# A state-space scan in two halves: carrying the state through the first token's inputs instead of through the scan's initial value

## The chip, the cores and the metric

The kernel runs on one core of a Trainium2 chip. A core has a matrix engine (TensorE, PE in the profile), a vector engine (VectorE, DVE), a scalar engine (ScalarE, ACT), a general engine (GpSimd, POOL), and SyncE (SP), whose queue issues the DMA transfers here. Each engine works through its own instructions in order; between engines, semaphores order the work. The metric is device microseconds for one execution of the whole program, and the median over runs is what counts.

## The reference

The input is `x` of shape (16, 256, 32, 32): 16 images (batches) of 256 channels and 1024 tokens. Two layers follow one another, each with a group norm ahead and a residual around it. Layer 0 is a transformer block: position embedding, layer norm, attention with 4 heads of 32, a second layer norm and a small feed-forward. Layer 1 is a Mamba block with a gate, and its core is a recurrence over the tokens, for 512 inner channels `d` with 64 states `n` each:

```
delta = softplus(dt @ dt_proj_w.T + dt_proj_b)
A = -exp(A_log)
def step(h, inp):                       # once per token, h0 = 0
    d_t, B_t, C_t, u_t = inp
    dA = exp(d_t[..., None] * A)
    h = dA * h + (d_t * u_t)[..., None] * B_t[:, None, :]
    y = einsum('bdn,bn->bd', h, C_t)
```

Per batch that is 512 x 64 = 32768 recurrences of 1024 steps. Each step multiplies the state by a decay `dA`, and adds an input `delta * u * B`. Everything is computed in 32-bit floats, but for the exact three-piece split of `delta` in bfloat16 that the kernel makes for one matmul.

## The kernel before

**The scan.** A scan instruction of VectorE runs one recurrence per partition along the free dimension: `h[c] = a[c] * h[c-1] + v[c]`. A scan here covers 128 partitions (64 states of 2 channels, interleaved) and 512 tokens. So 1024 tokens take two halves `t = 0` and `t = 1`, and 512 channels take 256 scans in each half. A *unit* is two scans (`e = 0, 1`), that is four channels; a batch has 256 units in the order `t`, `k` (channel block of 128), `q` (of 32), `i` (of 4), and all 16 batches make 4096 units and 8192 scans. The second half has to go on from where the first ended: after the units of one `(k, q)` ScalarE copies the last column of its 16 scans into the tile `last` (L895), and the scans of `t = 1` name a column of `last` as their initial value.

**What a unit needs.** `load` issues a DMA on SP that brings `delta * u` of its four channels to all partitions as `dub` (L832; seven buffers, each set free by the scans of its unit). `inputs` multiplies it by `B` in place, once per `e`, on GpSimd (L842). `decay` has TensorE spread `delta` over the partitions into PSUM (`a`, L851; four buffers) and ScalarE take the exp with the scale `acol`, which holds `A` (L854). `scan` runs the two scans (L864). `outputs` contracts the states with `C` on TensorE (L901, L913), with ScalarE copies, and SP stores the result.

**The order.** A loop over the units writes the program out, and a pass at the end fixes that order on PE, ACT, DVE and POOL. In the turn of unit n it issues the load of unit n+6 (`AHEAD`), the multiplies of unit n+4 (`LEAD`), the scans of n, the decay of n+2, a share of the *side work*, and a step of the outputs that are running. The side work is everything else for the next batch (first norm, attention, and `scan_inputs`, which prepares the scan's operands and stores them in DRAM) and `gate_and_store` of the batch before. It is a generator whose steps carry weights, spread evenly over the units. The last batch has only a `gate_and_store` beside it. Before the first scan the first batch's preparation runs alone.

**Lines that the change and the prediction touch.** In `scan_inputs`, for each channel block `d`, `delta` of both halves is finished by two subtractions (L716), ScalarE casts its first piece (L717), `du` is formed and stored for the loads (L721, L722), and the pieces are stored as `dps` (L733), from which each `(k, q)` later loads `pieces` (L826). At the start, `vec` brings all per-channel constants in one DMA (L113), and `a_neg` is the exp of its `A_log` columns (L141), which becomes `acol`.

Of the kernel before, what the change touches and what calls it, by code (L numbers as in the profile page):

```python
# [11 lines left out]
F32 = mybir.dt.float32  # L12
BF16 = mybir.dt.bfloat16
AF = mybir.ActivationFunctionType
ALU = mybir.AluOpType
# [4 lines left out]
P = 128  # L20
# [8 lines left out]
DI = 512  # L29
ND = DI // P  # L30
NS = 64
# [4 lines left out]
SLOTS = 16  # L36
# [12 lines left out]
NV = _n  # L49
# [3 lines left out]
def attention_then_scan_kernel(  # L53
# [18 lines left out]
    nc = tc.nc  # L72
    B = x.shape[0]

    def pool(name, bufs, **kw):
        return ctx.enter_context(tc.tile_pool(name=name, bufs=bufs, **kw))

    const = pool("const", 1)
# [4 lines left out]
    small = pool("small", 2)  # L83
    dutp = pool("dutp", 7)
    blk = pool("blk", 2)
    hst = pool("hst", 1)
    dram = pool("dram", 2, space=DRAM)
# [14 lines left out]
    def work(name, n=L):  # L102
        return wide.tile([P, L + 2 + CONV], F32, name=name, tag="wide")[:, :n]

    def hwork(name):
        return half.tile([P, HL], F32, name=name, tag="half")

    def hs(h):
        return ts(h, HL)


    vec = const.tile([P, NV], F32, name="vec")
    nc.sync.dma_start(vec, vecs)  # L113

    def col(name, i=0, n=1):
        o, w = _COLS[name]
        assert i + n <= w
        return vec[:, o + i : o + i + n]
# [19 lines left out]


    a_neg = work("a_neg", ND * NS)  # L140
    nc.scalar.activation(a_neg, col("A_log", 0, ND * NS), AF.Exp)  # L141
    nc.vector.tensor_scalar(a_neg, a_neg, -1.0, None, ALU.mult)
    acol = const.tile([P, DI // 2], F32, name="acol")
    a2 = work("a2", 2 * P).rearrange("p (j n i) -> p j n i", j=2, i=2)
# [32 lines left out]
    t = work("ones_s")[:1]  # L177
# [3 lines left out]
    for k in range(KC):  # L181
        t = work("rel_s").rearrange("p (i j) -> p i j", j=32)
# [122 lines left out]
    state = [dict() for _ in range(B)]  # L305
# [231 lines left out]
    def scan_inputs(b):  # L537
        st = state[b]
# [25 lines left out]
        zs = dram.tile([DI, L], F32, name="zs", tag="zs")  # L564
# [9 lines left out]
        for d in range(ND):  # L574
            z = work("z")
            for hf in range(2):
# [7 lines left out]
                t = hwork("z_t")  # L584
# [6 lines left out]
        ud = dram.tile([DI, L], F32, name="ud", tag="ud")  # L591
        gs = dram.tile([C, L], F32, name="gs", tag="gs")
# [80 lines left out]
        rows = dram.tile([2 * NS, L], F32, name="rows", tag="rows")  # L673
# [2 lines left out]

        dps = dram.tile([ND * 3 * P, L], BF16, name="dps", tag="dps")
        dus = dram.tile([ND * NT * P, TB], F32, name="dus", tag="dus")  # L680
        dpv = dps.rearrange("(k q e p x) t -> k p e q x t", k=ND, q=4, e=2, p=3)
# [2 lines left out]
        def begin(d, hf):  # L684
            ps = psum("d_ps")
            nc.tensor.matmul(ps, wdt_s[:, ts(d, P)], dt[:RANK, hs(hf)], start=True, stop=True)
            e = hwork("sp_e")
            nc.scalar.activation(e, ps, AF.Abs, bias=col("dt_b", d))
            nc.scalar.activation(e, e, AF.Exp, scale=-1.0)
            return ps, e  # L690
# [11 lines left out]
        items = [begin(0, 0)]  # L702
        yield 1
        for d in range(ND):
            items = [more(d, *items[0]), begin(d, 1)]
            yield 1
            items[1] = more(d, *items[1])
            rest(*items[0])
            yield 1.4
            rest(*items[1])  # L710
            for ps, e, s in items:
                nc.scalar.activation(s, s, AF.Ln)
            yield 1.7
            pc = [ptp.tile([P, L], BF16, name="pc", tag="pt") for _ in range(3)]
            for hf, (ps, e, s) in enumerate(items):
                nc.vector.tensor_tensor(ps, s, ps, ALU.subtract)  # L716
                nc.scalar.copy(pc[0][:, hs(hf)], ps)  # L717
            yield 1.4
            du = work("du")
            for hf, (ps, e, s) in enumerate(items):  # L720
                nc.vector.tensor_tensor(du[:, hs(hf)], us[d][:, hs(hf)], ps, ALU.mult)  # L721
            nc.sync.dma_start(duv[d], du.rearrange("d (t c) -> d t c", t=NT))  # L722
            yield 1.4
            for hf, (ps, e, s) in enumerate(items):
                nc.vector.tensor_tensor(ps, ps, pc[0][:, hs(hf)], ALU.subtract)
                nc.scalar.copy(pc[1][:, hs(hf)], ps)
            yield 1.4
            for hf, (ps, e, s) in enumerate(items):
                nc.vector.tensor_tensor(pc[2][:, hs(hf)], ps, pc[1][:, hs(hf)], ALU.subtract)
            items, ps, e, s = [], None, None, None  # L730
            for p in range(3):
                for e in range(2):
                    nc.sync.dma_start(dpv[d, p, e], pc[p][e:P:2])  # L733
            if d + 1 < ND:
                items = [begin(d + 1, 0)]
            yield 1.4
        st.update(zs=zs, gs=gs, ud=ud, rows=rows, dps=dps, dus=dus)
        st["ys"] = dram.tile([DI, L], F32, name="ys", tag="ys")
        yield 1

# [2 lines left out]
    def gate_and_store(b):  # L743
# [61 lines left out]
    units = [  # L805
        (b, t, k, q, i)
        for b in range(B) for t in range(NT) for k in range(ND) for q in range(4) for i in range(8)
    ]
    blocks, loaded, decays = {}, {}, {}
    now = {}  # L810
# [27 lines left out]
    def inputs(n):  # L838
        b, t = units[n][:2]
        for e in range(2):  # L840
            v = loaded[n][:, e, :]
            nc.gpsimd.tensor_tensor(v, v, blocks[b, t]["bt"], ALU.mult)  # L842

    def decay(n):
        b, t, k, q, i = units[n]
        pieces = blocks[b, t, k, q]
        decays[n] = [aps.tile([P, TB], F32, name="a", tag="a") for _ in range(2)]
        for e in (1, 0):
            a, r = decays[n][e], ds(64 * e, 48)
            w = pick[r, i].rearrange("p n j -> p (n j)")  # L850
            nc.tensor.matmul(a, w, pieces[r], start=True, stop=True)  # L851
        for e, a in enumerate(decays[n]):
            at = 64 * k + 16 * q + 2 * i + e
            nc.scalar.activation(a, a, AF.Exp, scale=acol[:, at : at + 1])  # L854

    def scan(n, e):
        b, t, k, q, i = units[n]
        if (i, e) == (0, 0):
            if (t, k, q) == (0, 0, 0):
                now["last"] = blk.tile([P, DI // 2], F32, name="last", tag="last")  # L860
            now["h", q % 2] = hst.tile([P, SLOTS, TB], F32, name=f"h{q % 2}", tag=f"h{q % 2}")
        at = 64 * k + 16 * q + 2 * i + e
        first = now["last"][:, at : at + 1] if t else 0.0
        nc.vector.tensor_tensor_scan(  # L864
            now["h", q % 2][:, 2 * i + e, :], decays[n][e], loaded[n][:, e, :], first,
            ALU.mult, ALU.add,
        )
        if e == 1:
            del decays[n], loaded[n]
# [3 lines left out]
    def spread_c(b, t):  # L873
        if t == 0:
            now["cd"] = hst.tile([P, TB // 16, P], F32, name="cd", tag="cd")
            nc.gpsimd.memset(now["cd"], 0.0)
        ct = blocks[b, t]["ct"].rearrange("p (a c e) -> p a c e", c=4, e=4)
        for c in range(4):
            for j in range(2):
                nc.scalar.activation(  # L880
                    now["cd"][:, :, 40 * c + j : 40 * c + j + 7 : 2], ct[:, :, c],
                    AF.Identity, scale=par[:, j : j + 1],
                )
# [58 lines left out]
    for n in range(2):  # L942
        decay(n)
    running = []
    side, rate, due = iter(()), 0.0, 0.0
    for n, (b, t, k, q, i) in enumerate(units):
        at = n % UNITS
        if at == 0:
            parts = [prepare(b + 1)] if b + 1 < B else []
            total = steps * len(parts)  # L950
            if b > 0:
                parts = [first_norm(b + 1), gate_and_store(b - 1), attention_layer(b + 1), scan_inputs(b + 1)]
                if b + 1 == B:
                    parts = parts[1:2]
                total += GATE
            side = chain(*parts)
            rate, due = total / (UNITS - AHEAD - 3), 0.0
        if at == UNITS - AHEAD:
            for _ in side:
                pass  # L960
            if b + 2 < B:
                for go in fetches(state[b + 2].setdefault("x", []), x[b + 2]):
                    go()
        if n + AHEAD < len(units):
            load(n + AHEAD)
        if n + LEAD < len(units):
            inputs(n + LEAD)
        scan(n, 0)
        scan(n, 1)
        if n + 2 < len(units):  # L970
            decay(n + 2)
        if at >= (1 if b + 1 < B else 8):
            due += rate
            while due > 0.0:
                due -= next(side, 1e9)
        for g in list(running):
            if next(g, g) is g:
                running.remove(g)
        if i == 0 and n > 0:
            g = outputs(*units[n - 1][:4])  # L980
            next(g)
            running.append(g)
        if (k, q, i) == (0, 0, 6):
            spread_c(b, t)
    for g in running:
        for _ in g:
            pass
# [7 lines left out]
    last = {}  # L995
# [65 lines left out]
```

## Time and profile before

| | us |
|---|---|
| median of 3 runs | 13833.62 (13815.34 to 13842.49) |
| the profiled execution | 13784.86 |
| its span, first to last instruction | 13782.7 |
| first scan starts, last one ends | 392.9, 13737.4 |
| a usual batch, first half / second half (batch 5) | 416 / 431 |
| the last batch, first half / second half | 361 / 315 |

The halves are cut at the start of their first scan. In the profile a group is one line, engine and operation with its tiles and shapes; behind the count stand the busy time of the group, the mean length of one instruction in nanoseconds, and after the bar the time in which its engine was idle just before such instructions, with what ended that idle time. `x4096: 1157/1197/1226` gives a group's minimum, median and maximum in nanoseconds. A wait that several semaphores ended is put down to the one that came last by the profile, so the releaser named isn't always the true one. Some records are missing, so counts can be a few short.

### The profile page before, as it was taken

How to read it: one execution, taken by the hardware profiler on the slowest of the kernel's cores; microseconds unless marked ns; L12 is line 12 of the kernel's file. 1: busy time of each engine (PE TensorE's matmuls, PEld its weight loads, DVE VectorE, ACT ScalarE, POOL GpSimd, SP SyncE). 2: the span in 40 equal slices, each digit the busy share in tenths (PEclk: the TensorE clock that was granted, in tenths of full speed). 3: DMA queues.
4: the chain of work that ended last, by engine and by line, in shares of the span. 5: the costliest groups of instructions: out<-in, count | busy, mean ns of one | idle time of the engine just before them, and what ended most of it. 6: DMA issues, size and time to landing. Idle time of an engine off the chain costs nothing. (4 is left out here: it accounts for less than half of the span.)

```text
span 13782.7 us, 435036 instructions
## 1 busy us (share of the span) xinstructions
PE 11113.2 (81%) x185744; PEld 5728.7 (42%) x185744; DVE 12135.5 (88%) x11699; ACT 8088.7 (59%) x14245; POOL 10477.2 (76%) x8214
## 2 busy tenths in 40 slices
PE   7787878878787787978879788797887978878767
PEld 3344444444444444444444444444444444434434
DVE  3898898898898889888898888889888898888898
ACT  3666665656655565655656655566555655556644
POOL 0787777777787777777777787777777777777788
PEclk8686767867777686876767777677776776867767
DMA  1566566565665656556565565656656565565666
GB/s 55 196 207 230 187 214 208 201 222 196 211 207 199 218 201 223 194 199 218 197 231 186 197 226 191 232 185 202 219 191 230 187 214 205 194 228 187 209 219 223
DMA packets 964174, 2804.18 MB, mean 203 GB/s; under 512 B 138162, under 2 KB 285747, under 8 KB 962228
## 3 DMA queue, kind: packets, MB, share of 16 engines
q1 hardware_dynamic: 962228, 2776.34, 58.8%
q8 instruction: 1452, 23.79, 0.7%
q14 instruction: 494, 4.05, 0.1%
HBM read 2514.18 MB, written 261.62 MB: 201 GB/s over the span
## 5 line engine op out<-in xcount | busy, mean ns | idle before, releaser
L842 POOL TENSOR_TENSOR dub<-dub,bt 128x512 f32<-128x512 f32 x8192 | 10422.4, 1307 | 3254.5 <-DMA dub<-dus 2878.4
L854 ACT ACTIVATE a<-a,acol 128x512 f32<-128x512 f32 x8192 | 5064.9, 660 | 3728.2 <-PE a L851 3689.1
L864 DVE TENSOR_TENSOR_SCAN h<-a,last,dub 128x512 f32<-128x512 f32 x4096 | 4932.9, 1261 | 227.0 <-POOL dub L842 128.8
L864 DVE TENSOR_TENSOR_SCAN h<-a,dub 128x512 f32<-128x512 f32 x4096 | 4700.9, 1201 | 276.7 <-POOL dub L842 186.6
L851 PE MATMUL a<-pieces,pick 48*128 48x512 bf16 x8192 | 2914.9, 480 | 2103.1 <-DVE h L864 2037.8
L901 PEld LDWEIGHTS yb<-h,cd 128*32 128x32 f32 x131072 | 2677.2, 140 | 2166.2 <-issue 1847.3
L901 PE MATMUL yb<-h,cd 128*32 128x64 f32 x131072 | 3090.5, 265 | 160.9 <-DVE yb L891 115.9
L851 PEld LDWEIGHTS <-pick 48*128 48x128 bf16 x8192 | 498.0, 96 | 2507.4 <-issue 2293.2
L408 PE MATMUL s_ps<-ka,qa 32*128 32x512 f32 x2048 | 1115.7, 1009 | 23.2 <-DVE mx L399 15.2
L399 DVE TENSOR_REDUCE mx<-s_ps 128x1 f32<-128x512 f32 x1024 | 654.9, 678 | 279.0 <-PE s_ps L408 278.2
L913 PEld LDWEIGHTS yb<-turn,y 128*16 128x16 f32 x32768 | 418.9, 120 | 960.3 <-ACT y L909 484.6
L909 ACT COPY y<-yb 128x256 f32<-128x256 f32 x1024 | 383.4, 374 | 693.6 <-PE yb L901 688.3
L913 PE MATMUL yb<-turn,y 128*16 128x32 f32 x32768 | 555.2, 216 | 193.8 <-ACT y L909 173.0
L444 PE MATMUL st_ps<-qa,ka 33*128 33x512 f32 x2048 | 590.2, 613 | 25.9 <-ACT pt L452 25.5
L432 PE MATMUL av<-pt,vv 128*64 128x512 f32 x2048 | 572.7, 635 | 4.3 <-ACT sums L390 3.3
L452 ACT ACTIVATE pt<-st_ps 128x512 f32<-128x512 f32 x1024 | 558.9, 609 | 28.8 <-PE st_ps L444 28.4
L408 PEld LDWEIGHTS s_ps<-ka,qa 32*128 32x128 f32 x2048 | 345.4, 274 | 402.3 <-DVE mx L399 221.4
L630 PE MATMUL g_ps<-w,xp 128*128 128x256 f32 x1536 | 475.2, 468 | 0.0
L630 PEld LDWEIGHTS g_ps<-w,xp 128*128 128x128 f32 x1536 | 401.9, 329 | 137.6 <-issue 92.6
L789 PE MATMUL m_ps<-w,xs 128*128 128x256 f32 x1024 | 316.7, 459 | 10.9 <-DVE xs L764 10.9
L921 ACT COPY yo<-yb 128x256 f32<-128x256 f32 x512 | 193.1, 377 | 222.2 <-PE yb L913 219.7
L615 DVE SCALAR_TENSOR_TENSOR u<-up,cwh,u 128x1024 f32<-128x1024 f32 x192 | 300.9, 1567 | 23.8 <-ACT u L607 23.6
(135 smaller groups left out, 7593.8 us busy)
## 6 DMA issues: line engine op xcount, KB each, us to landing
dub<-dus SPq DMA_DIRECT2D x4096, 512.0 KB
dps<-pc SPq DMA_DIRECT2D x384, 128.0 KB
pieces<-dps SPq DMA_DIRECT2D x1024, 48.0 KB
xs<-in_x_dram SPq DMA_DIRECT2D x64, 512.0 KB
xs<-kept SPq DMA_DIRECT2D x64, 512.0 KB
zs<-z SPq DMA_DIRECT2D x64, 512.0 KB
ud<-u SPq DMA_DIRECT2D x64, 512.0 KB
dus<-du SPq DMA_DIRECT2D x64, 512.0 KB
```

What stands on the lines that cost most here:

```text
L399: nc.vector.tensor_reduce(mx[:, e, c, hf : hf + 1], s, AX.X, ALU.max)
L408: nc.tensor.matmul(s, qa[r, ts(c, P)], ka[r, hs(hf)], start=True, stop=True)
L432: nc.tensor.matmul(av[ts(e, 2 * DH)], vv[j // (NJ // 2)][:, j % (NJ // 2), 2 * pair + e, :], pts[e], start=(j == 0), stop=(j == NJ - 1),)
L444: nc.tensor.matmul(s, ka[r, ts(j, P)], qa[r, hs(hf)], start=True, stop=True)
L452: nc.scalar.activation(pt, s, AF.Exp)
L630: nc.tensor.matmul(ps[:, ts(q, C)], xp[k][:, ds(first + t, P, 4)], wg_s[:, k, t, :], start=(i == 0), stop=False,)
L842: nc.gpsimd.tensor_tensor(v, v, blocks[b, t]["bt"], ALU.mult)
L851: nc.tensor.matmul(a, w, pieces[r], start=True, stop=True)
L854: nc.scalar.activation(a, a, AF.Exp, scale=acol[:, at : at + 1])
L864: nc.vector.tensor_tensor_scan(now["h", q % 2][:, 2 * i + e, :], decays[n][e], loaded[n][:, e, :], first, ALU.mult, ALU.add,)
L901: nc.tensor.matmul(yb[ts(g, 32), ts(s, 64)], cd[:, at // 16, ts(c, 32)], hbuf[:, :, at : at + 4], start=(c == 0), stop=(c == 3),)
L913: nc.tensor.matmul(out4[32 * s : 32 * s + 16, half, e], y2[:, 64 * s + e : 64 * s + 64 : 4], turn[:, e], start=True, stop=True,)
```

## The change

All scans start from the constant 0.0. What the initial value did for the second half is done by its first token's input instead: for `h[0] = a[0] * last + v[0]` the product `a[0] * last` is added to `v[0]` ahead of the scan. So the kernel needs the decay of token 512 for every channel and state. `scan_inputs` has ScalarE copy `delta` of that token for each block of 128 channels, and stores it in a small DRAM tensor `d0`. In the batch's own turn, while the first half is scanned, two DMAs spread `d0` over the partitions as `ea`, GpSimd multiplies it by `acol`, and ScalarE takes the exp (at the first units of `k = 1` with `q = 0, 1, 2`). In the second half GpSimd multiplies 16 columns of `ea` and `last` into `on` for each `(k, q)`, and adds two columns of it to the first token of `dub` for each unit, after the unit's two multiplies.

The space for `ea` comes from `vec`, which no longer holds the `A_log` columns: these are loaded straight into `a_neg`, by a DMA of their own.

```diff
+    NC = NV - ND * NS
+    vec = const.tile([P, NC], F32, name="vec")
+    nc.sync.dma_start(vec, vecs[:, :NC])
...
     a_neg = work("a_neg", ND * NS)
-    nc.scalar.activation(a_neg, col("A_log", 0, ND * NS), AF.Exp)
+    nc.sync.dma_start(a_neg, vecs[:, NC:])
+    nc.scalar.activation(a_neg, a_neg, AF.Exp)
...
+        d0 = dram.tile([DI, 1], F32, name="d0", tag="d0")
+        dcol = small.tile([P, ND], F32, name="dcol", tag="dcol")
...
                 nc.vector.tensor_tensor(ps, s, ps, ALU.subtract)
                 nc.scalar.copy(pc[0][:, hs(hf)], ps)
+            nc.scalar.copy(dcol[:, d : d + 1], items[1][0][:, :1])
+            nc.sync.dma_start(d0[ts(d, P), :], dcol[:, d : d + 1])
             yield 1.4
...
             nc.gpsimd.tensor_tensor(v, v, blocks[b, t]["bt"], ALU.mult)
 
+        if t == 1:
+            k, q, i = units[n][2:]
+            if i == 0:
+                at = 64 * k + 16 * q
+                now["on"] = small.tile([P, SLOTS], F32, name="on", tag="on")
+                nc.gpsimd.tensor_tensor(
+                    now["on"], now["ea"][:, ds(at, SLOTS)], now["last"][:, ds(at, SLOTS)], ALU.mult
+                )
+            v = loaded[n][:, :, 0]
+            nc.gpsimd.tensor_tensor(v, v, now["on"][:, ds(2 * i, 2)], ALU.add)
...
-        at = 64 * k + 16 * q + 2 * i + e
-        first = now["last"][:, at : at + 1] if t else 0.0
         nc.vector.tensor_tensor_scan(
-            now["h", q % 2][:, 2 * i + e, :], decays[n][e], loaded[n][:, e, :], first,
+            now["h", q % 2][:, 2 * i + e, :], decays[n][e], loaded[n][:, e, :], 0.0,
             ALU.mult, ALU.add,
         )
...
+        if (t, k, i) == (0, 1, 0):
+            if q == 0:
+                now["ea"] = hst.tile([P, DI // 2], F32, name="ea", tag="ea")
+                src = state[b]["d0"].rearrange("(m j s) x -> j m (s x)", m=16, j=2)
+                for j in range(2):
+                    nc.sync.dma_start(
+                        now["ea"][j:P:2].rearrange("p (m s) -> p m s", m=16),
+                        src[j].unsqueeze(0).to_broadcast([NS, 16, 16]),
+                    )
+            elif q == 1:
+                nc.gpsimd.tensor_tensor(now["ea"], now["ea"], acol, ALU.mult)
+            elif q == 2:
+                nc.scalar.activation(now["ea"], now["ea"], AF.Exp)
```

More of the change, by code (lines that the diff above doesn't have):

```diff
@@ L109, in hs @@
         return ts(h, HL)
-    vec = const.tile([P, NV], F32, name="vec")
-    nc.sync.dma_start(vec, vecs)
+    NC = NV - ND * NS
+    vec = const.tile([P, NC], F32, name="vec")
+    nc.sync.dma_start(vec, vecs[:, :NC])
     def col(name, i=0, n=1):
@@ L736, in scan_inputs @@
             yield 1.4
-        st.update(zs=zs, gs=gs, ud=ud, rows=rows, dps=dps, dus=dus)
+        st.update(d0=d0, zs=zs, gs=gs, ud=ud, rows=rows, dps=dps, dus=dus)
         st["ys"] = dram.tile([DI, L], F32, name="ys", tag="ys")
```

## The prediction

> **What bounds the kernel now.** First the page: busy shares and the cost of the groups; for the two scan rows I took the answer by form, which names every releaser.
>
> ```profile
> PE 11113.2 (81%) x185744; PEld 5728.7 (42%) x185744; DVE 12135.5 (88%) x11699; ACT 8088.7 (59%) x14245; POOL 10477.2 (76%) x8214
> ...
> L842 POOL TENSOR_TENSOR dub<-dub,bt 128x512 f32<-128x512 f32 x8192 | 10422.4, 1307 | 3254.5 <-DMA dub<-dus 2878.4
> ...
> L864 DVE TENSOR_TENSOR_SCAN h<-a,last,dub 128x512 f32<-128x512 f32 x4096 | 4932.9, 1261 | 227.0 <-POOL dub L842 128.8 <-issue 94.5
> L864 DVE TENSOR_TENSOR_SCAN h<-a,dub 128x512 f32<-128x512 f32 x4096 | 4700.9, 1201 | 276.7 <-POOL dub L842 186.6 <-issue 83.4 <-ACT a L854 1.4
> ```
>
> The reader is to see that VectorE (DVE) is the fullest engine, that 9633.8 us of its 12135.5 are scans, and that the scans which name `last` (second half of the tokens) are 60 ns longer on average than those that start from the constant. GpSimd (POOL) comes next; its idle time is mostly waiting for loads, whose buffers only finished scans set free. Then the scan line alone:
>
> ```profile
> L864 DVE TENSOR_TENSOR_SCAN h<-a,dub x4096: 1157/1197/1226, 392.9 to 13421.2; 128x512 f32<-128x512 f32 x196
> L864 DVE TENSOR_TENSOR_SCAN h<-a,last,dub x4096: 1153/1257/1285, 780.2 to 13736.1; 128x512 f32<-128x512 f32 x196
> ```
>
> The medians (third field: min/median/max) differ by 60 ns and each form is narrow, so the 60 ns belong to the form, not to some disturbed stretch. Whether they are real pace or only a longer record, the timeline tells, from unbroken rows of scans and multiplies (start, length, count):
>
> ```profile
> 4013.33 11.25 DVE L864 TENSOR_TENSOR_SCAN h<-a,dub 128x512 f32<-128x512 f32 x10 [1.27 <-POOL dub L842]
> ...
> 13639.61 10.65 DVE L864 TENSOR_TENSOR_SCAN h<-a,last,dub 128x512 f32<-128x512 f32 x9
> ...
> 13639.91 11.20 POOL L842 TENSOR_TENSOR dub<-dub,bt 128x512 f32<-128x512 f32 x9
> ```
>
> Less one scan, over the steps between: (11.25-1.20)/9 = 1.117 us from the constant, (10.65-1.26)/8 = 1.174 us from `last`, so 57 ns of pace. A multiply: (11.20-1.27)/8 = 1.241 us. A unit (two of each) is 2.23 or 2.35 us of DVE and 2.48 us of POOL. Where DVE does scans alone, POOL is already the slower of the two. So the last view is by stage: batch 5's second half, its first 16 units, and batch 15's second half (us, then busy of each engine, PE's granted clock, DMA).
>
> ```profile
> 4988.20:5419.00 430.80, 332.99 (x5684) 173.92 (x5684) 393.06 (x369) 263.03 (x450) 318.35 (x249) 0.74 0.61 205
> ...
> 4988.40:5033.50 45.10, 37.05 (x717) 17.36 (x715) 43.44 (x41) 31.37 (x62) 40.68 (x34) 0.81 0.62 210
> ...
> 13422.30:13737.40 315.10, 235.67 (x5437) 139.11 (x5436) 307.93 (x267) 174.89 (x311) 303.16 (x246) 0.70 0.66 226
> ```
>
> A usual second half is DVE's (393 of 431 us; POOL 318). The last one, with no next batch to prepare, is a tie (308 and 303 of 315, ten POOL records missing).
>
> **What the Trainium skill says.** "VectorE: DVE Perf Modes", section "Scalar operands", says that a scalar is a constant in the instruction or a [P, 1] operand read per partition; it prices neither, this trace does. "SBUF — State Buffer", section "Who interferes with whom", says that a VectorE instruction with one SBUF input doesn't contend with GpSimd and one with two does; the scan reads `a` from PSUM, and the narrow spread of both forms beside a busy POOL agrees. "GPSIMD Engine Reference", section 3.1, has 4497 ns for an fp32 tensor_tensor of 2048 elements. No run here has a short one.
>
> **The change part by part.** *Scans.* 4096 lose 60 ns: 245.8 us at most. 256 of them are in the last half, counted below; 3840 give 15 x 15.4 = -230 us.
>
> *The small adds.* 2048 of 128x2 and 256 multiplies of 128x16 on POOL; none is in the trace. From 1.241 us at 512 elements and the skill's 4.497 us at 2048: 2.12 ns an element, 0.156 us fixed, so an estimate of 0.16 us. The add reads what the multiply before it wrote, and may wait for it to end: up to one overlap more, 1.271-1.241 = 0.03. I take 0.20 for both kinds (0.25 for the multiply). Below: 0.10, the 128x1 memset on POOL (99 to 103 ns). Above: 0.40, the 294 ns of the 128x128 select in the preamble and 0.1 for a wait on each side. A usual half then needs 318 + 128x0.2 + 16x0.25 = 348 us of POOL in about 418: hidden under DVE. If the cover were gone it would be 30 us a half. No scan starts until the add of its unit is done; multiplies are issued four units ahead, so that is late only where POOL has no lead.
>
> *Where it has little.* The first 8 units of a second half fall in the attention's value phase, with no VectorE work but scans: POOL 8 x 2.68 = 21.4 us against DVE 8 x 2.23 = 17.9. The difference, 3.6 us, comes partly out of the lead; I charge half, 1.8 x 15 = +27.
>
> *The last half.* POOL sets it: 128 x 2.48 + 26 + 4 = 347 us, less the four units that it is ahead at the start (10), so 337 and a scan pair: about 338 against 315.1, +23. At 0.10 it is +10, at 0.40 +50.
>
> *Waits on other engines.* Where VectorE waits for an answer of PE or ScalarE asked for a unit earlier (the waits for `z_t`, `d_ps`, `ln_v`, `ln_m`, `gn_v_ps`: about 16 in a second half), a unit shorter by 0.12 us is a wait longer by as much: 16 x 0.12 x 15 = +29.
>
> *ScalarE.* Per batch four 128x1 copies, at most 0.22 each (the 128x16 copy of `last` takes 0.217), and one exp of 128x256 (0.42, the row at L141): 1.3 us on an engine 59% busy. It runs beside other exps, so no table load. Hidden.
>
> *DMA and its queue.* Four stores of `d0` a batch, each of 128 pieces of 4 bytes. Each waits on SP for a ScalarE copy behind two casts behind two 0.68 us VectorE subtractions: the next `dub` load is issued some 2.3 us later, and `pieces` behind it. Four of 256 loads; they come six units (20 us) before their scan, and the store of `du` blocks the queue likewise today. Two loads of `ea` a batch, 2048 pieces of 64 bytes; the skill ("DMA: Bandwidth & Descriptors", "Specifications") wants 512 bytes for full rate. No run shows this one; from 0 to 8 us of queue, at a unit where POOL is waiting for loads anyway. The `ea` multiply on POOL takes 256 x 2.12 ns + 0.16 = 0.70 us. Together I charge 0.6 us a batch, +10; 0 to 60 is the range.
>
> *Preamble.* `a_neg` gets its own DMA: 0.4 us of SP issue and perhaps a microsecond of landing, +1.
>
> Sum: -230 + 27 + 23 + 29 + 10 + 1 = -140. The profiled span of 13782.7 (13784.9 with what lies around it) becomes 13643. The runs' median, 13833.6, lies 49 us above that execution; I take the 140 from it: 13693.
>
> **The rivals.** *All of it hidden* (adds of 0.10, no lengthened waits): -230 + 10 + 5 = -215, about 13620. For it: VectorE is 91% busy in these halves. Against it: the last half can't gain.
>
> *The chain scan, PE `a`, exp, scan takes over.* A scan's end frees the PSUM buffer that PE refills and ScalarE turns into the decay two units on. If it has too little slack, a wait takes the place of the 60 ns: with half of the gain left, and the 29 of lengthened waits within the other half, -115 + 61 = -54, about 13780. For it: PE is 81% busy at a clock of 0.73. Against: scans waited 1.4 us in all for that exp.
>
> *GpSimd becomes the bound, slower than before.* Place: the small add; price: from 0.65 us each. At that price a usual half needs 318 + 83 + 11 = 412 us of POOL, level with DVE's 415, stretches without VectorE side work go over and eat some 10 of the 15.4 us, and the last half loses 128 x 0.65 + 11 - 10 = 85, which is what the 15 others then gain. At 0.8 us: POOL needs 434 in each of 15 halves (3 more than now and bursts of 5), the last +105: +225, about 14060. For it: an instruction of two elements is all fixed cost, and two dependences per unit. Against: memsets of 0.1 us.
>
> *The 60 ns aren't the operand's*: then only costs remain, +60, 13890. The first-half scans, which are the new form exactly, speak against it.
>
> **How the numbers follow.** Chances: forecast 0.68 (13640 to 13750), all hidden 0.14, chain 0.08, GpSimd bound 0.07, not the operand 0.03. Leaving out the last two, half the chain's and a third of the first rival's gives 13625 to 13775. Within 0.2% of 13834 (28 us, about what this kernel's measurement can tell) lies some half of the chain's case and a little of GpSimd's: 0.05. Faster 0.87, slower 0.08.
>
> **What would show it.** One scan group of 8192 with mean near 1201 ns; a 128x2 add row near 0.2 us; second halves near 419 us, the last near 338 with scans waiting for the add; first halves unchanged. An add above 0.4 us, or scans waiting for `a`, would make the forecast wrong.

## The result and the profile after

The changed kernel takes 13928.94 us (median of 4 runs, 13919.26 to 13938.57) against 13838.06 for the kernel before (4 runs). The ratio is 1.0067, with a 95% interval of 1.0050 to 1.0085: it is slower by about 93 us, where 13693 was forecast. The profiled execution has a span of 13936.7 us, 154.0 above that of before.

First the page of the changed kernel (busy shares), its scan line, and the answer by form for its GpSimd instructions. As in before's rows, the bar parts busy time and mean from the idle time just ahead.

```profile
PE 11167.3 (80%) x185744; PEld 5754.2 (41%) x185744; DVE 11952.6 (86%) x11699; ACT 8103.0 (58%) x14325; POOL 10982.3 (79%) x10534
...
L879 DVE TENSOR_TENSOR_SCAN h<-a,dub x8192: 1153/1198/1226, 428.7 to 13890.1; 128x512 f32<-128x512 f32 x200
...
L859 POOL TENSOR_TENSOR dub<-dub,on 128x2 f32<-128x2 f32 x2048 | 475.8, 232 | 160.5
L855 POOL TENSOR_TENSOR on<-ea,last 128x16 f32<-128x16 f32 x256 | 60.7, 237 | 0.0
L1010 POOL TENSOR_TENSOR ea<-ea,acol 128x256 f32<-128x256 f32 x16 | 11.7, 730 | 0.0
```

All scans now have a median of 1198 ns: the 60 ns are gone, as forecast. VectorE is busy 183 us less, and not the 246 of 4096 times 60 ns: the scans' own rows give 215 (9633.8 us before, 9418.5 now), and its other instructions grew by 32 us, for a reason that no run isolates. The small adds take 232 ns and 78 ns of idle time ahead of each (160.5 us over 2048), so some 0.27 us once the overlap of 0.046 us between neighbouring records is taken off; 0.20 was forecast. In the trace, a unit whose multiplies follow one another without waiting takes GpSimd 2.45 us without an add and 2.72 with one, the same 0.27. The time is longer for all that. The stages, cut as before (us, then busy of PE, PE's weight loads, DVE, ACT, POOL; PE's granted clock, DMA share, GB/s): the second half of batch 5, its last 16 units and the last half, first before (whose last half stands in the prediction), then after.

```profile
4988.36:5419.49 431.13, 333.23 (x5685) 173.87 (x5683) 393.19 (x369) 263.36 (x450) 318.68 (x250) 0.74 0.61 205
...
5377.84:5419.49 41.65, 29.86 (x672) 17.08 (x672) 41.29 (x39) 22.75 (x42) 31.76 (x27) 0.62 0.76 267
```

```profile
5080.04:5514.14 434.10, 333.31 (x5684) 173.92 (x5682) 378.52 (x369) 263.98 (x454) 354.62 (x391) 0.74 0.64 203
...
5466.25:5514.14 47.89, 33.53 (x671) 17.82 (x671) 40.29 (x39) 23.37 (x43) 40.48 (x47) 0.50 0.66 238
13543.73:13891.35 347.62, 253.76 (x5437) 143.66 (x5436) 303.96 (x267) 175.46 (x311) 334.70 (x392) 0.64 0.62 205
```

VectorE has 14.7 us less to do in the half, and the half is 3 us longer; its last 16 units alone are 6.2 us longer, at a lower transfer rate (238 GB/s for 267). The last half grew from 315.0 to 347.6 us and is GpSimd's now. The 154 us of the two profiles lie so, by the starts of the scans: before the first scan +35.8; batch 0's halves +12.8 and +2.3; the 14 first halves of batches 1 to 14 +1.7 each (+23), the 14 second halves +4.0 each (+57); batch 15 -9 and +33.

Of the 35.8 us ahead of the first scan, some 21 are not the change's. In the first 300 us TensorE was granted 0.83 of its clock in the profile of before and 0.76 in this one, and executions of other kernels here start near one or the other as well. The row kernel below, whose start is the same but for the stores, had 0.84 and its first scan at 393.6; without adds, which this stretch doesn't have, it had 0.76 and 414.1. So 14 to 15 us of it are left for the stores, and totals of single executions are compared with care.

Then the queue that issues the transfers (SP), at the same step of the preparation of batch 0, before and after:

```profile
376.36 0.38 SPq L722 DMA_DIRECT2D dus<-du  x1
376.83 6.07 SPq L733 DMA_DIRECT2D dps<-pc  x6
```

```profile
404.98 0.33 SPq L723 DMA_DIRECT2D d<-dcol  x1
406.22 0.38 SPq L728 DMA_DIRECT2D dus<-du  x1
407.45 12.06 SPq L739 DMA_DIRECT2D dps<-pc  x6
```

The six stores of `dps` behind a store of `d0` take 12.06 us to issue instead of 6.07. The transfer queue of the whole run, before and after (packets, MB, share of the 16 DMA engines):

```profile
q1 hardware_dynamic: 962228, 2776.34, 58.8%
```

```profile
q1 hardware_dynamic: 1004868, 2778.48, 61.9%
```

By the trace, packets were in flight for 8623 us of all 16 engines instead of 8110. The 2 MB more are the loads of `ea`; the 64 stores bring 0.03 MB. If all of the 513 us were theirs, it would be 8 us for each; the experiments will put it at some 6. The waits of SP name them too: in the changed kernel it waited 67.5 us at the loads of `dub` and 46.7 at the stores of `dps` for the landing of `d<-dcol`.

### The profile page after: what moved, and what is told of

It reads as the page before. It is cut to its first block, busy times and chain, and to the rows that moved or that the text cites. A ratio compares the mean times of both kernels' runs of the same rounds, so it can differ in the third digit from the quotient of the medians.

```text
span 13936.7 us, 435942 instructions
## 1 busy us (share of the span) xinstructions
PE 11167.3 (80%) x185744; PEld 5754.2 (41%) x185744; DVE 11952.6 (86%) x11699; ACT 8103.0 (58%) x14325; POOL 10982.3 (79%) x10534
## 5 line engine op out<-in xcount | busy, mean ns | idle before, releaser
L879 DVE TENSOR_TENSOR_SCAN h<-a,dub 128x512 f32<-128x512 f32 x8192 | 9418.5, 1203 | 665.2 <-issue 236.4
L446 PE MATMUL st_ps<-qa,ka 33*128 33x512 f32 x2048 | 604.5, 625 | 27.1 <-ACT pt L454 26.5
L859 POOL TENSOR_TENSOR dub<-dub,on 128x2 f32<-128x2 f32 x2048 | 475.8, 232 | 160.5
```

Of the source, the lines that this page charges most:

```text
L446: nc.tensor.matmul(s, ka[r, ts(j, P)], qa[r, hs(hf)], start=True, stop=True)
L879: nc.vector.tensor_tensor_scan(now["h", q % 2][:, 2 * i + e, :], decays[n][e], loaded[n][:, e, :], 0.0, ALU.mult, ALU.add,)
```

## The experiments

Theory S puts the loss to the 4-byte stores of `d0`, and otherwise keeps the forecast. Rival G puts it to GpSimd's adds and the scans' waits for them. Rival C is the chain of the forecast's rivals: a shorter scan only waits longer for TensorE and the exp.

**The stores as one row.** The store in the channel loop goes; behind the loop:

```diff
-            nc.sync.dma_start(d0[ts(d, P), :], dcol[:, d : d + 1])
...
+        row = psum("d0_ps", 1)
+        for d in range(ND):
+            nc.tensor.matmul(row[:, ts(d, P)], dcol[:, d : d + 1], ident, start=True, stop=True)
+        drow = hwork("drow")[:1]
+        nc.scalar.copy(drow, row)
+        nc.sync.dma_start(d0, drow)
```

> The changed kernel, but the first-half delta column of a batch is turned into one row by four tiny TensorE matmuls and stored with a single contiguous 2 KB DMA, instead of four stores of 128 pieces of 4 bytes. Theory S (each 4-byte store stops the DMA rings for some 7 us, and the loads behind it come late): 64 stops go, the rest of the forecast's sum holds, so about 120 us below the kernel before (80 to 160), first scan within 5 us of 393, DMA share back near 59%. Rival G (GpSimd's adds and the scans' waits for them ate the gain): the stores do not matter, still some 60 to 90 us above the kernel before. Rival C (faster scans only wait longer for TensorE and ScalarE): within 30 us of the kernel before.

Measured: 13771.78 us against 13809.7, ratio 0.9977 (0.9968 to 0.9987). The first scan starts at 393.6. From 1.0067 to 0.9977 is 0.90%, some 124 us, and it falls where the stores were. But S is only half right: 32 us of gain, not 120, which is close to the 30 that rival C allowed.

**The stores alone.** The kernel before, with these two lines in the channel loop and nothing that reads `d0`:

```diff
+            nc.scalar.copy(dcol[:, d : d + 1], items[1][0][:, :1])
+            nc.sync.dma_start(d0[ts(d, P), :], dcol[:, d : d + 1])
```

> The kernel before plus only the ScalarE copy of a delta column and its 4-byte store, four per batch; nothing reads what is stored. Theory S: 36 us before the first scan, 13 in the first half of batch 0, and some 6 to 10 in each of 14 second halves, together 120 to 200 us above the kernel before. Rivals G and C, and the forecast's own term: the stores are hidden, at most 15 us above.

Measured: ratio 1.0081 (1.0058 to 1.0105), some 112 us, for four small copies and four stores a batch. DMA share 61.7%. The expected 120 to 200 took the 21 us of TensorE's clock for the stores'; without them the total lies in the range, but a second half is longer by 3.5 us (433.2 for 429.7) and not by the 6 to 10 expected, so what a stop costs depends on the work around it. G and C fall as explanations of the slowdown.

**Without the adds.** The row kernel, less the adds:

```diff
-            nc.gpsimd.tensor_tensor(v, v, now["on"][:, ds(2 * i, 2)], ALU.add)
```

> The row store, with the 2048 small GpSimd adds left out, so the second half does not receive the carried state (that part of the computation is missing); scans start from the constant. Theory S: the full gain of the scans less the lengthened waits, 180 to 220 us below the kernel before, and 30 to 60 below the row store with adds, mostly in the last half. Rival G: this one alone is fast, more than 150 below the row store. Rival C: within 50 us of the kernel before.

Measured: 13711.69 us, ratio 0.9935 (0.9919 to 0.9950), some 90 us below, where 180 to 220 were expected. The scans are as short as they can be here (mean 1201 ns), GpSimd has no adds, the stores are gone, and less than half of the scans' time comes back. S is right with 30 to 60 us below the row store (it is 58) and wrong with its gain; G wanted more than 150 below the row store, and C at most 50 below the kernel before. The stages say where. Mean us of these units over batches 1 to 14, from the starts of the scans:

| units of a batch | before | changed | row | row, no adds | selective (below) |
|---|---|---|---|---|---|
| 128 to 135 | 19.9 | 19.9 | 19.9 | 19.9 | 20.0 |
| 136 to 143 | 26.3 | 28.7 | 28.5 | 28.4 | 26.6 |
| 144 to 191 | 176.2 | 171.2 | 171.4 | 170.8 | 171.1 |
| 192 to 215 | 83.3 | 82.8 | 82.8 | 82.6 | 83.9 |
| 216 to 239 | 82.4 | 83.2 | 80.3 | 80.3 | 80.3 |
| 240 to 255 | 41.6 | 48.0 | 42.7 | 40.8 | 42.3 |
| second half | 429.7 | 433.8 | 425.5 | 422.8 | 424.1 |

Every 8 units hold 16 scans, so 0.96 us could be gained there. Without adds, units 144 to 191 give 5.4 us of 5.8, units 216 to 239 give 2.1 of 2.9, and units 240 to 255 give 0.9 of 1.9; the first 8 give nothing, units 136 to 143 lose 2.1 (3.1 with what they should have gained), units 192 to 215 give 0.7 of 2.9. 6.9 us of 15.4 are left. Kernels whose second halves differ only by stores that stop nothing (below) have 429.5 to 430.3 us for 429.7, so a few tenths are spread. The changed kernel's column differs from the row's from unit 216 on, by 8.2 us: there the channel blocks' stores of `d0` stand, and the loads of the next batch wait behind them.

Why the first 8 units give nothing shows in the timeline of the kernel without adds, in batch 5, by engine (start, length, what, idle time ahead and its releaser): VectorE, then ScalarE, TensorE and GpSimd.

```profile
5010.30 2.34 DVE L885 TENSOR_TENSOR_SCAN h<-a,dub 128x512 f32<-128x512 f32 x2 [0.20 <-issue]
5013.52 2.34 DVE L885 TENSOR_TENSOR_SCAN h<-a,dub 128x512 f32<-128x512 f32 x2 [0.89 <-POOL dub L854]
```

```profile
5012.44 0.37 ACT L930 COPY y<-yb 128x256 f32<-128x256 f32 x1 [0.66 <-PE yb L922]
5012.77 2.39 ACT L877 ACTIVATE a<-a,acol 128x512 f32<-128x512 f32 x4
```

```profile
5009.31 1.02 PE L446 MATMUL st_ps<-qa,ka 33*128 33x512 f32 x4
5010.27 1.08 PE L434 MATMUL av<-pt,vv 128*64 128x512 f32 x4
5011.27 1.10 PE L922 MATMUL yb<-h,cd 128*32 128x64 f32 x64
5012.31 0.39 PE L874 MATMUL a<-pieces,pick 48*128 48x512 bf16 x2
```

```profile
5010.60 4.97 POOL L854 TENSOR_TENSOR dub<-dub,bt 128x512 f32<-128x512 f32 x4 [0.72 <-DMA dub<-dus]
```

The scans at 5013.52 waited 0.89 us, put down to POOL. But TensorE worked without a gap from the attention's `st_ps` and `av` to `yb`; only then came `a` (5012.31 to 5012.70), though the scan that frees its buffer, four scans back, had ended at 5008.98. The exp behind it began at 5012.77, its first instruction takes 0.66 us, and the scan followed 0.09 us after. The scan's own multiply had ended 10.7 us earlier. The releaser named is the wrong one, and it is so nearly everywhere. In batches 1 to 14 of this kernel the scans idled 501 us; 498 of them ended within 0.15 us of the end of the scan's own exp, and 0.4 within 0.15 us of the end of its own multiply. For the kernel before it is 437 of 452 us for the exp, and none for the multiply. That the exp came last is thus counted; why it came late is shown by the timeline for this one place.

**The adds alone.** The kernel before, with adds of zero in the same place:

```diff
+        if t == 1:
+            v = loaded[n][:, :, 0]
+            nc.gpsimd.tensor_tensor(v, v, zero, ALU.add)
```

> The kernel before plus 2048 GpSimd adds of zero of the same shape and place, scans still from the kept state. Theory S: hidden in 15 second halves (at most 2 us each), and about 30 in the last one, so 25 to 60 us above the kernel before. Rival G: 150 us or more above. Rival C says nothing on this one.

Measured: ratio 1.0017 (1.0010 to 1.0024), 23 us. A second half takes 430.1 us for 429.7, the last one 344.3 for 315.0. So the adds are hidden but in the last half. Beside the faster scans they cost more: from 0.9935 without them to 0.9977 with them is 58 us; in the profiles 27 us in the last half and 2.7 in each of the 14 others. That is near the 50 us that the forecast charged for adds (27 and 23), so G doesn't explain the missing gain either.

**What stops the transfers.** The kernel before again with the stores alone, once into rows that lie 512 bytes apart, once with pieces of 64 bytes:

```diff
-        d0 = dram.tile([DI, 1], F32, name="d0", tag="d0")
+        d0 = dram.tile([DI, P], F32, name="d0", tag="d0")
...
-            nc.sync.dma_start(d0[ts(d, P), :], dcol[:, d : d + 1])
+            nc.sync.dma_start(d0[ts(d, P), :1], dcol[:, d : d + 1])
```

```diff
+        d0 = dram.tile([DI, 16], F32, name="d0", tag="d0")
+        dcol = small.tile([P, ND, 16], F32, name="dcol", tag="dcol")
...
+            nc.scalar.copy(dcol[:, d], items[1][0][:, :16])
+            nc.sync.dma_start(d0[ts(d, P), :], dcol[:, d])
```

> The kernel before plus the 4-byte stores, but each of the 128 pieces goes to its own 512-byte row of DRAM. Theory L (the stop comes from many short writes into the same few hundred bytes): the stop is gone, transfer in the ten microseconds behind a store as ahead of it (about 200 GB/s), time within 20 us of the kernel before. Theory P (short pieces stop the rings wherever they go): as with the packed store, 50 to 140 GB/s in the bins 2 to 10 us behind it, and 90 to 140 us above the kernel before.

> The kernel before plus four stores a batch of 128 pieces of 64 bytes, packed (8 KB). Theory L: eight pieces share 512 bytes instead of 128, so the stop shrinks to a small part, at most 30 us above the kernel before. Theory P: half or more of the packed 4-byte store's 110 us stays, since a piece of 64 bytes is still short.

One execution each gave 13837.11 and 13825.98 us beside one of the kernel before of 13765.14, outside what L had said; yet no stop showed. So both were run again, 12 times each.

> The 4-byte stores into rows 512 bytes apart, timed: one look put it 72 us above one look of the kernel before, though no stop shows behind the stores. Theory L: the difference was the spread of single runs, so within 25 us of the kernel before. Theory P: 90 to 140 us above, and the stop is hidden from the packets' times.

> The packed stores of 64-byte pieces, timed. Theory L: within 30 us of the kernel before. Theory P: 55 us or more above.

Measured: ratios 1.0003 (0.9995 to 1.0012) and 1.0010 (0.9996 to 1.0024); DMA share 59.3% in both. The same number of packets (971444 in the whole run) costs nothing measurable with rows of their own, and 112 us packed into 512 bytes. Packets were in flight 404 us of all 16 engines longer with the packed store (8593 for 8189), 6.3 us for each of the 64. Three stretches of 3 us, from 3 to 12 us behind the same store (the second of the four in batch 4's turn), show it, with the columns of the stages above (the last two are the DMA share and GB/s): the changed kernel, then the rows 512 bytes apart.

```profile
4558.30:4561.30 3.00, 2.92 (x66) 1.80 (x66) 3.00 (x5) 2.23 (x4) 2.92 (x5) 0.50 1.64 152
4561.30:4564.30 3.00, 2.56 (x68) 1.80 (x66) 3.00 (x4) 1.24 (x2) 2.52 (x3) 0.50 0.78 128
4564.30:4567.30 3.00, 2.82 (x14) 0.73 (x12) 3.00 (x4) 1.99 (x4) 1.46 (x2) 0.50 0.67 122
```

```profile
4520.20:4523.20 3.00, 2.54 (x66) 1.80 (x66) 3.00 (x5) 1.92 (x4) 0.00 (x0) 0.50 0.98 287
4523.20:4526.20 3.00, 2.43 (x58) 1.49 (x60) 3.00 (x3) 1.55 (x3) 2.49 (x2) 0.50 0.98 357
4526.20:4529.20 3.00, 3.00 (x29) 0.87 (x21) 3.00 (x5) 1.61 (x3) 2.01 (x2) 0.50 0.71 239
```

About half the rate or less, with a share that goes over 1 in one stretch: packets stay in flight for longer. On the mean over all 64 stores, the rate from 6 to 10 us behind the store's issue is 47 GB/s in the changed kernel and 304 with the rows apart, while the engines are as busy in both (0.94 and 0.89). From 2 us before a store to 12 us after it, 37 packets longer than 0.7 us begin on the mean, against 6 with the rows apart; the longest takes 6.3 us in the median store, against 1.1.

**TensorE relieved.** To see whether TensorE sets the pace at units 192 to 207, where the gate's convolution runs, two kernels with a third of its matmuls: the kernel before, and the row kernel without adds.

```diff
-            for i in range(3 * KC):
+            for i in range(2):
```

> The kernel before with only 2 of the 6 matmuls of each gate convolution block (the gate's other taps and channels are missing from the result). It is the control for the next one. If TensorE sets the pace at units 192 to 207 of a batch, these 16 units get shorter (55.3 us before) by a microsecond or more.

> The row store without the adds (the carried state is missing), with the same 2 of 6 gate matmuls. Theory C (behind a full TensorE the exp comes late, so a shorter scan only waits): with TensorE relieved the scans' 0.96 us per 8 units come back at units 192 to 207, 1.5 us or more for the 16 units against the control, where it was 0.4 with all six matmuls; elsewhere no change. Rival W (the wait there is another engine's or a fixed latency): still at most 0.7.

Measured in one execution each, for units 192 to 207 (mean of batches 1 to 14): 55.3 us before, 52.9 in the control; 54.9 without adds, 51.0 with TensorE relieved as well. The shorter scan is worth 0.4 us with all matmuls and 1.9 with a third of them. At units 184 to 191, the convolution's start, it goes from 1.1 to 1.8. So TensorE holds back gain here, as C said, and W's at most 0.7 is missed. But the rest of C's picture isn't shown: at units 200 to 207 alone the control has 24.8 us and so has the other, and all 1.9 us came at 192 to 199, where the scans alone save 0.96. TensorE was also relieved by less than the edit suggests. For units 192 to 207 of batch 5, before and in the control:

```profile
5211.83:5267.27 55.44, 48.27 (x766) 30.37 (x766) 51.30 (x43) 27.59 (x49) 43.93 (x32) 0.94 0.63 206
```

```profile
5220.62:5272.47 51.85, 46.62 (x726) 24.21 (x725) 48.56 (x42) 27.38 (x48) 43.59 (x31) 0.73 0.67 219
```

The granted clock fell from 0.94 to 0.73, and TensorE's busy time hardly did. For a whole second half, the shorter scan is worth 8.5 us with TensorE relieved (425.8 less 417.4) and 6.9 without, so this stage accounts for some 1.5 of the 8.5 us that are lost.

For units 136 to 143 no run was made for this alone; their wait is for the transfer of the softmax sums. VectorE waited for it 26.5 us in the kernel before, 23.4 with the adds alone and 29.3 in the selective kernel below, which all keep the old scans there, and 63.2, 59.0 and 60.2 in the changed, the row and the row kernel without adds. So the wait follows the shorter scans, not the adds; why it grows by more than they save is open.

**A version that beats both.** The row store; the zero start and its add only where the table shows a gain, and elsewhere `last` as the initial value:

```diff
+    def added(n):
+        b, t, k, q, i = units[n]
+        return b + 1 < B and (144 <= n % UNITS < 192 or 216 <= n % UNITS < 240)
...
-        if t == 1:
+        if added(n):
...
+        at = 64 * k + 16 * q + 2 * i + e
+        first = now["last"][:, at : at + 1] if t and not added(n) else 0.0
```

> The row store, and the zero start with its add only at units 144 to 191 and 216 to 239 of the first 15 batches, where VectorE sets the pace; all other scans of second halves start from the kept state as before. Theory S with C: 72 of 128 units a half keep their 0.7 to 0.8 us per 8 units (6.7 a half, 100 in all), the last half costs nothing more, the added loads and the ends about 10: 60 to 110 us below the kernel before and below the row store everywhere. Rival G: the adds eat it, within 20 of the kernel before.

Measured: 13705.39 us against 13811.39, ratio 0.9930 (0.9912 to 0.9947), some 97 us faster than the kernel before: 0.7% below it, and 1.4% below the changed kernel.

```profile
L891 DVE TENSOR_TENSOR_SCAN h<-a,dub 128x512 f32<-128x512 f32 x6256 | 7187.6, 1202 | 332.0 <-POOL dub L858 215.4 <-issue 105.5 <-ACT a L881 1.8
L891 DVE TENSOR_TENSOR_SCAN h<-a,last,dub 128x512 f32<-128x512 f32 x1936 | 2320.2, 1260 | 173.6 <-POOL dub L858 87.5 <-issue 84.0
...
L869 POOL TENSOR_TENSOR dub<-dub,on 128x2 f32<-128x2 f32 x1080 | 249.8, 231 | 84.7
```

1080 adds instead of 2048 keep the gain of the kernel without any. The last half takes 311.4 us.

## Why the prediction was wrong

The forecast said 13693 (13625 to 13775) and gave 0.87 to faster. By its own steps:

- **Scans: right.** 60 ns are off the median of each. The pace from start to start, in unbroken rows of six scans or more in second halves, went from 1.176 to 1.117 us.
- **DMA and its queue: the step that turned the sign.** It charged 10 us for all transfers, with 0 to 60 as range, and put the four stores of `d0` down as one late load of `dub` each, hidden by six units of lead. Counting pieces and bytes missed what they do to the rest: each holds up the other transfers of the core, for some 6 us by the DMA share. Measured alone: 112 us, and 124 in place. The upper part of the range was meant for the loads of `ea`, which did no visible harm: with them and the row store, first halves take 419.6 us, and 417.6 to 419.9 in kernels without them.
- **Waits on other engines: right in kind, too small by four.** 1.9 us a half was charged for about 16 waits of the side work. 8.5 of 15.4 us were lost without any adds, some 120 us over the 15 halves in place of 29. The step gave each wait the 0.12 us of one unit and counted only side work that waits for TensorE or ScalarE. It had neither the wait for the transfer of the softmax sums (3.1 of the 8.5 us lie in its stage) nor the scans themselves behind a full TensorE, which are shown for about 1.5 us by the relieved kernels and for the first 8 units by one timeline; the cause of the rest is open.
- **The chain as a rival was dismissed on a misread row.** Against it the forecast held that scans waited 1.4 us in all for the exp. That was by the releaser's name. The same rows gave 315 us to POOL and 178 to "issue", and nearly all of those ended with the exp. The first row of scans that the forecast quoted shows the misnaming: 1.27 us "<-POOL dub L842", but that multiply had ended 9.8 us before the scan began, and the exp 0.4 us before. With the stores out of the way, the row kernel's 32 us of gain lie nearer to the 54 of this rival than to the 140 of the forecast.
- **The place of little lead: wrong cause, small size.** The first 8 units were charged 1.8 us for GpSimd. They lose 0.96 with or without adds, so not to GpSimd; by the timeline it is TensorE.
- **Adds and the last half: right in mechanism, small by 10 us.** 0.27 us an add for 0.20, 348 us for 338. In the changed kernel's last half the scans idled 43 us, and 42 of these ended within 0.15 us of the end of the unit's own add. In the other halves adds cost 2.7 us each where the sum had them hidden beyond the 1.8.
- **The preamble** was charged 1 us; the stores of batch 0's preparation cost 14 to 15 there.

By contrasts of the ratios: scans without adds -90, adds +58, stores +124. Their sum is the measured change by construction, since each contrast starts where the last one ended; the stores' 112 us beside the kernel before are the independent check. "GpSimd becomes the bound", the rival on the slower side, gave the right sign for a wrong reason: it needed adds of 0.65 us.

## What to carry to other kernels

Price a small store by where its pieces go, and look at the transfers behind it: here 128 short pieces into one stretch of 512 bytes of DRAM slowed the other transfers to a sixth for some microseconds, rows apart cost nothing measurable, and one contiguous row took the loss away. When a trace names a releaser that had long been done, compute the slack to each input of the waiting instruction (here the end of the exp against the start of the scan) before a rival is dismissed. And here a faster instruction on the fullest engine was worth its saving only in the stages where that engine had few waits; a change that trades it for work elsewhere can be put into those stages alone.

## What the runs showed of the hardware

A store of 128 pieces of 4 bytes into 512 contiguous bytes of DRAM held up the other transfers of the core, for 6.3 us by the DMA share (47 GB/s instead of 304 from 6 to 10 us behind it); into rows 512 bytes apart, or as 64-byte pieces packed in 8 KB, the same 128 pieces showed no such stop (ratios 1.0003 and 1.0010). The Trainium skill says in "DMA: Bandwidth & Descriptors", section "Specifications", that below 512 bytes a transfer is a read and a write back; that such round trips into the same few hundred bytes wait for one another fits, but no run here shows the mechanism, and the spaced 4-byte pieces show that shortness alone isn't it. A scan of 128x512 with its initial value from a column took 60 ns longer than one from a constant (medians of 1257 and 1197 ns, start to start 1.176 and 1.118 us in unbroken rows of the kernel before). A GpSimd tensor_tensor of 128x2 took 232 ns and held the engine for about 0.27 us behind the multiply whose result it reads. The forecast had estimated 0.16 us for it ahead of any wait, from the 4497 ns for 2048 elements in the Trainium skill's "GPSIMD Engine Reference", section 3.1, and this trace's multiply; the record was half as long again. The estimate's slope of 2.12 ns an element does agree with this trace: 730 ns at 256 elements and 1271 at 512 make 2.11.
